# A bidirectional gated recurrence with fusion and a ternary FFN: the recurrent part's fixed slots become a list-scheduled graph of tasks

## Chip, cores and metric

One core of one Trainium2 chip runs the whole kernel in one launch. The metric is device time in microseconds (us), the median of several executions. The engines are named as in the profile: PE (TensorE matmul) and PEld (its weight load), DVE (VectorE), ACT (ScalarE), POOL (GpSimd) and SP (SyncE, which issues most DMAs).

## What is computed

Eight batches of 512 tokens with 512 features, fp32. A four-layer gated recurrence (forward and backward, with the same weights), a fusion of both directions, a residual, then an FFN with ternary weights:

```python
def _mingru(x, Wz, bz, Wh, bh):
    z = jax.nn.sigmoid(jnp.einsum('bsi,hi->bsh', x, Wz) + bz)
    h_tilde = jnp.tanh(jnp.einsum('bsi,hi->bsh', x, Wh) + bh)
    a = jnp.clip(1.0 - z, CLAMP_LO, CLAMP_HI)
    return _linear_scan(a, z * h_tilde)
...
    for i in range(L):
        h_new = _mingru(h, Wz[i], bz[i], Wh[i], bh[i])
        if i > 0:
            h_new = h_new + h
        h = _layernorm(h_new, gamma, beta)
...
h_fwd = _stack(x, ...)
h_bwd = jnp.flip(_stack(jnp.flip(x, axis=1), ...), axis=1)
return jnp.einsum('bsi,hi->bsh', jnp.concatenate([h_fwd, h_bwd], -1), fusion_W) + fusion_b
...
# FFN: absmean(W) is W made ternary (-1, 0, 1) at half the mean of abs(W)
h = jax.nn.gelu(jnp.einsum('btd,hd->bth', x, absmean(W_fc)), approximate=False)
h = layernorm(h, ln_w, ln_b)
return jnp.einsum('bth,dh->btd', h, absmean(W_proj))
...
x = x + recurrent(layernorm(x))
x = x + ffn(layernorm(x))
```

The call passes one weight for `Wz` and `Wh` and for both directions (`ctx_1024`) and one bias (`cond_1024`), so one product serves the sigmoid and the tanh, and layer 0's product serves both directions.

## The kernel before

**Layout.** Within the recurrence a state is held with features on partitions: four tiles of 128 features by 512 tokens. A *gate* is one such output tile: four fp32 matmuls (L487; L535 for layer 0), accumulated in one PSUM bank `u`. From `u`, ACT makes `a` (sigmoid of the negated sum), `t` (tanh) and `z` (sigmoid), L505 to L507; POOL clamps `a` (L511); DVE multiplies `z` by `t` (L514), runs the scan along the tokens (L518) and from layer 1 on adds the old state (L588, L594).

**Layer norm.** It needs rows, so each of four token tiles is turned (four transposes, L316) into a bank `pt`. DVE finds mean and variance (L171, L173), adds epsilon (L177), negates the mean (`nmu`, L182); POOL raises to the power -1/2 (L178); ACT makes `nmr` = -mean times that power (L188) and writes the normalised rows `tok` (L189). When the four are there, four groups of transposes turn them back (L325, bank `pf`) and ACT applies gamma and beta (L331). Of the last layer only the statistics are needed (`rsv`), since the norm is folded into the fusion weights `fw`; of three of its sixteen sequences ACT finds them in two passes (L396, L398). The norm of the input is likewise folded into layer 0: its rows give a scale per token (`rx`, then `scale` by way of `pr`, L385), which DVE multiplies into `u` (L546).

**Fusion.** For a token tile, four matmuls for each direction into `pu` (L622), two evictions by DVE that scale and add to the residual row (L632), and a store to `x1` in DRAM.

**Order.** Batches go in pairs. Within a pair, layers 1 to 3 run over (first batch, forward), (first, backward), (second, forward), (second, backward), four gates each. The fusion tiles of a pair alternate with the layer-0 gates of the next. The order of everything around the gates is written out by hand as *slots*: `slot` (one gate or one fusion tile) issues its matmuls, then what is due of `stages` (factors, clamps, scans, sums) and shares of the queues `turns` and `backs` (transposes and what follows them). How late a step comes is a count of slots. Each engine carries out its own instructions in the order in which they were issued. PSUM's eight banks are divided: four for `u` and `pu`, two for `pt`, two for `pf`.

**Side work.** While the first pair runs, both FFN weights are read in 32 parts, summed in absolute value by ACT (L653), read again, made ternary by DVE (L193, L194) and stored; they come back as `fcq` and `pwq` at the end of the recurrent part. `fold_sums`, `fold_parts`, `fold` and `fold_bias` put gamma, beta and the mean into `fw` and `fb`.

**FFN.** For each batch 16 chunks of 128 hidden features: eight matmuls into `ph` (L910), gelu, square and a split into `ghi` and `glo` (ACT and DVE, L914 to L927), and two chunks later eight matmuls into `po` (L937). The next batch's rows are read, their statistics found (`stats`) in chunks 6 and 7, normalised in 8 and 9 and turned in the last four.

Of the kernel before, what the change touches and what calls it, by code (L numbers as in the profile page):

```python
# [12 lines left out]
ALU = mybir.AluOpType  # L13
# [11 lines left out]
def kernel(  # L25
# [17 lines left out]

# [9 lines left out]
    ZT = 16  # L61
    TOK = 10

    const = ctx.enter_context(tc.tile_pool(name="const", bufs=1))
    small = ctx.enter_context(tc.tile_pool(name="small", bufs=8))
    wpool = ctx.enter_context(tc.tile_pool(name="wts", bufs=1))
    hp = ctx.enter_context(tc.tile_pool(name="h", bufs=6))
    dram = ctx.enter_context(tc.tile_pool(name="x1", bufs=1, space=bass.MemoryType.DRAM))

    tokp = ctx.enter_context(tc.tile_pool(name="tok", bufs=TOK))  # L70
    xsp = ctx.enter_context(tc.tile_pool(name="xs", bufs=12))
    zp = ctx.enter_context(tc.tile_pool(name="z", bufs=ZT))
    ps_f = ctx.enter_context(tc.tile_pool(name="ps_f", bufs=2, space=PSUM))
# [4 lines left out]
    stgp = rec.enter_context(tc.tile_pool(name="stg", bufs=3))  # L78
    qp = rec.enter_context(tc.tile_pool(name="quant", bufs=2))


# [5 lines left out]
    x1 = [[dram.tile([P, H], F32, tag=f"x1_{b}_{t}", name=f"x1_{b}_{t}") for t in range(NT)] for b in range(B)]  # L87


    gw = [wpool.tile([P, NC_, H], F32, tag=f"w{l}", name=f"gw{l}") for l in range(L)]  # L90

    xs = {}

    def load_x(use, b, t):
        xs[use, b, t] = xsp.tile([P, H], F32, tag="xs", name=f"x{use}_{b}_{t}")
        nc.sync.dma_start(out=xs[use, b, t], in_=x[b, ts(t, P), :])

    def load_gw(l):
        nc.sync.dma_start(out=gw[l], in_=gru_wT[l].rearrange("(c p) h -> p c h", p=P))

    xT = {}

    def load_xT(b):
        xT[b] = hp.tile([P, NC_, S], F32, tag="h", name=f"xT_{b}")
        nc.sync.dma_start(out=xT[b], in_=xt[b].rearrange("(c p) s -> p c s", p=P))
# [15 lines left out]
    for i in range(2):  # L121
        plain = tokp.tile([P, H], F32, tag="tok", name=f"plain{i}")[:, 0:P]
        nc.vector.memset(plain, 0.0)
        nc.vector.memset(plain[64 * i : 64 * i + 1, :], 1.0 / H if i else 1.0)
        s = fusp.tile([P, P], F32R, name=f"fpick{i}")
        nc.vector.tensor_copy(s, plain)
        picks.append(s)


    xT[0] = hp.tile([P, NC_, S], F32, tag="h", name="xT_0")  # L130
# [4 lines left out]
    def first_xT(q, c):  # L135
        q.dma_start(out=xT[0][:, c, :], in_=xt[0][ts(c, P), :])

    def first_rows(q, t):
        xs["n", 0, t] = xsp.tile([P, H], F32, tag="xs", name=f"xn_0_{t}")
        q.dma_start(out=xs["n", 0, t], in_=x[0, ts(t, P), :])  # L140
# [10 lines left out]
    for t in range(NT):  # L151
        load_x("n", 1, t)
    load_xT(1)
# [3 lines left out]
    for l in range(1, L):  # L157
        load_gw(l)
# [7 lines left out]
    ngb = const.tile([P, L, NC_], F32, name="ngb")  # L166

    def stats(src, name, rs=None, shift=True):

        st = small.tile([P, 6], F32, tag="st", name=f"st_{name}")  # L170
        nc.vector.bn_stats(st, src)  # L171
        mv = small.tile([P, 2], F32, tag="mv", name=f"mv_{name}")
        nc.vector.bn_aggr(mv, st)  # L173
        if rs is None:
            rs = small.tile([P, 1], F32, tag="rs", name=f"rs_{name}")
        ve = small.tile([P, 1], F32, tag="ve", name=f"ve_{name}")
        nc.vector.tensor_scalar(ve, mv[:, 1:2], LN_EPS, None, ALU.add)  # L177
        nc.gpsimd.tensor_tensor(rs, ve, mhalf, ALU.pow)  # L178
        if not shift:
            return rs, None  # L180
        nmu = small.tile([P, 1], F32, tag="nmu", name=f"nmu_{name}")
        nc.vector.tensor_scalar(nmu, mv[:, 0:1], -1.0, None, ALU.mult)  # L182
        return rs, nmu

    def normalise(dst, src, rs_nmu, name):
        rs, nmu = rs_nmu
        nmr = small.tile([P, 1], F32, tag="nmr", name=f"nmr_{name}")
        nc.scalar.activation(nmr, nmu, AF.Copy, scale=rs)  # L188
        nc.scalar.activation(dst, src, AF.Identity, bias=nmr, scale=rs)  # L189

    def ternary(dst, w, hi_lo):

        nc.vector.tensor_scalar(dst, w, hi_lo[1], None, ALU.is_lt)  # L193
        nc.vector.scalar_tensor_tensor(dst, w, hi_lo[0], dst, ALU.is_gt, ALU.subtract)  # L194

    def fc_part(i):

        return fc_wT[ts(i % NC_, P), ts(i // NC_, 512)]

    def proj_part(i):  # L200
        return proj_wT[ts(i, P), :]

    def load_y(b):

        for t in range(NT):
            xs["y", b, t] = xsp.tile([P, H], F32, tag="xs", name=f"xy_{b}_{t}")
            nc.sync.dma_start(out=xs["y", b, t], in_=x1[b][t])

    ys = {}

    def y_chunk(b, toks, c, px):

# [3 lines left out]
        def split():  # L216
            hi = zp.tile([P, S], F32R, tag="z", name=f"yhi_{b}_{c}")
            lo = zp.tile([P, S], F32R, tag="z", name=f"ylo_{b}_{c}")
            nc.scalar.copy(hi, px)
            nc.vector.tensor_tensor(lo, px, hi.bitcast(F32), ALU.subtract)  # L220
            ys.setdefault(b, []).append((hi, lo))
        return split

    NW = NQ * NC_
    fcq, pwq = [], []
    rows = {}


    with rec:
        gp = rec.enter_context(tc.tile_pool(name="gate", bufs=3))  # L230
        ps_u = rec.enter_context(tc.tile_pool(name="ps_u", bufs=4, space=PSUM))
        ps_t = rec.enter_context(tc.tile_pool(name="ps_t", bufs=2, space=PSUM))


        nc.scalar.activation(warm, warm, AF.Sigmoid)

        now = [0]
        state = {}
        rsv = {}
        turns, backs = [], []  # L240

        held = [0]

        class Tokens(list):


            lag = 1

            def append(self, tile_):
                super().append(tile_)  # L250
                self.at = now[0] + self.lag

        def ready(at):
            if isinstance(at, Tokens):
                return len(at) == NT and at.at <= now[0]
            return at <= now[0] and held[0] < TOK

        def shares(cap):


            last = []
            for q in (turns, backs):
                some = []
                for i in range(max(2, cap)):
                    if not q or not ready(q[0][0]):
                        break
                    at, piece = q[0][:2]
                    late = (at.at if isinstance(at, Tokens) else at) + piece <= now[0]
                    if i >= cap and not late:
                        break  # L270
                    some.append(take(q))
                last = some + last
            return last

        zlive = [0]

        left = {}

        def queue(q, key, at, piece, go):
            left[key] = left.get(key, 0) + 1  # L280
            q.append((at, piece, key, go))

        def take(q):
            _, _, key, go = q.pop(0)
            left[key] -= 1
            return go()

        def need(*keys):

            while any(left.get(k) for k in keys):  # L290
                slot(None, 2)

        def tokens(source, tok, rs, name):

            def go():
                src = source()
                found = stats(src, name, rs, tok is not None)
                if tok is None:
                    return lambda: None
                held[0] += 1  # L300

                def last():
                    tile_ = tokp.tile([P, H], F32, tag="tok", name=f"tok_{name}")
                    normalise(tile_, src, found, name)
                    tok.append(tile_)
                return last
            return go

        def turned(zs, t, name, frees=0):
            def source():  # L310
                if t == NT - 1:
                    zlive[0] -= frees
                spare = name.startswith("00_0") and t > 1
                pt = (ps_f if spare else ps_t).tile([P, H], F32, tag="pf" if spare else "pt", name=f"pt_{name}")
                for c in range(NC_):
                    nc.tensor.transpose(pt[:, ts(c, P)], zs[c][:, ts(t, P)], ident)  # L316
                return pt
            return source

        def back(toks, dst, c, affine, name):  # L320

            def go():
                pf = ps_f.tile([P, S], F32, tag="pf", name=f"pf_{name}")
                for t in range(NT):
                    nc.tensor.transpose(pf[:, ts(t, P)], toks[t][:, ts(c, P)], ident)  # L325
                if c == NC_ - 1:
                    held[0] -= NT
# [524 lines left out]
        load_pw(3)  # L852

# [239 lines left out]
```

## Time and profile before

| | |
|---|---|
| median of three runs | 1712.43 us (1712.39 to 1712.62) |
| the profiled execution: device time | 1712.95 us |
| its span, first to last instruction | 1711.2 us |
| first gate starts | 8.71 us |
| first FFN matmul starts | 1217.46 us |
| busy: DVE / ACT / POOL | 1389.1 / 1089.5 / 377.2 us |
| gates of layers 1 to 3 (L487), busy | 345.5 + 345.5 us |
| fusion matmuls (L622), busy | 115.2 + 115.1 us |

The span is what the trace shows of one execution; the device time has a little around it. A window line gives a stretch's start and end, its length, and for each engine the busy time and the number of instructions (in brackets), then the granted PE clock, the share of the DMA engines and GB/s. A wait line gives the waiting engine, the tile it works on and its line, what released it, and then the sum in us, the number of waits and the longest. In a timeline the two numbers ahead of the engine are start and duration in us; matmuls overlap in the pipeline, so the distance of starts, not the duration, is their pace.

### The profile page before, as it was taken

Reading aid. Unit: us, or ns where it says so; the run is one execution under the profiler, and the core shown is the slowest. Engines: PE = TensorE matmul, PEld = TensorE weight load, DVE = VectorE, ACT = ScalarE, POOL = GpSimd, SP = SyncE. Lnnn points to the kernel's source line nnn. Section 1 sums busy time; section 2 is a strip of 40 time slices with the busy share of each in tenths; the row PEclk is TensorE's granted clock in tenths of the full one; section 3 lists DMA queues with packets and bytes.
Section 4 is the critical chain, followed back from the end, with each engine's and each line's share of the span. In section 5 each row is a group of like instructions: output and inputs, shape, how many; then the busy total and the mean of one; then the engine's idle time right before and its main releaser. Section 6 shows DMA issues by size and latency. Waiting matters only on the chain.

```text
span 1711.2 us, 19776 instructions
## 1 busy us (share of the span) xinstructions
PE 1700.3 (99%) x6440; PEld 1042.6 (61%) x6440; DVE 1389.1 (81%) x2619; ACT 1089.5 (64%) x1918; POOL 377.2 (22%) x558
## 2 busy tenths in 40 slices
PE   9999999999999999999999999999999999999999
PEld 5455554555555455555545555554688888888887
DVE  7988889889887888888788888885568768768877
ACT  5898873468886346888535688862356566666654
POOL 3333333223332222333222222321000000000000
PEclk9999999999999999999999999999999999999999
DMA  7002231150000125000012200102201101100100
GB/s 271 19 25 81 98 93 37 66 193 19 13 1 1 56 68 191 19 13 1 1 56 75 98 28 22 75 1 99 74 1 50 50 1 50 50 21 30 50 19 31
DMA packets 46599, 91.75 MB, mean 54 GB/s; under 512 B 5280, under 2 KB 5536, under 8 KB 45472
## 3 DMA queue, kind: packets, MB, share of 16 engines
q1 hardware_dynamic: 45488, 88.78, 15.1%
q10 hardware_dynamic: 1008, 1.70, 0.3%
q8 instruction: 51, 0.84, 0.2%
q14 instruction: 52, 0.43, 0.1%
HBM read 65.30 MB, written 25.17 MB: 53 GB/s over the span
## 4 chain that ended last, share of the span: by engine, by line
PE 92%; DVE 5%; ACT 2%; POOL 1%; issue 0%; DVEq 0%
PE u L487 33%; PE po L937 14%; PE ph L910 14%; PE pu L622 13%; PE u L535 6%; PE pt L316 6%; PE pf L325 4%; DVE z L518 1%; PE py L214 1%; DVE z L514 1%; DVE st L171 1%; ACT tok L189 1%; DVE z L588 1%; PE pst L948 0%; POOL rs L178 0%
## 5 line engine op out<-in xcount | busy, mean ns | idle before, releaser
L487 PE MATMUL u<-xT,gw 128*128 128x512 f32 x768 | 345.5, 593 | 0.0
L487 PE MATMUL u<-h,gw 128*128 128x512 f32 x768 | 345.5, 592 | 0.0
L518 DVE TENSOR_TENSOR_SCAN z<-a,z 128x512 f32<-128x512 f32 x224 | 277.1, 1237 | 21.8 <-DVE z L514 0.9
L511 POOL TENSOR_SCALAR a<-a 128x512 f32<-128x512 f32 x224 | 150.3, 671 | 559.2 <-ACT a L505 558.3
L487 PEld LDWEIGHTS u<-xT,gw 128*128 128x128 f32 x768 | 138.6, 190 | 138.7 <-issue 137.0
L487 PEld LDWEIGHTS u<-h,gw 128*128 128x128 f32 x768 | 138.6, 190 | 138.2 <-issue 138.2
L505 ACT ACTIVATE a<-u,ngb 128x512 f32<-128x512 f32 x192 | 131.7, 686 | 142.4 <-PE u L487 140.9
L937 PE MATMUL po<-pwq,ghi 128*128 128x512 f32 x512 | 202.8, 396 | 0.0
L171 DVE BATCH_NORM_STATS2 st<-pt 128x6 f32<-128x512 f32 x244 | 169.3, 694 | 39.2 <-PE pt L316 32.5
L937 PE MATMUL po<-pwq,glo 128*128 128x512 f32 x512 | 199.7, 390 | 0.0
L910 PE MATMUL ph<-yhi,fcq 128*128 128x512 f32 x512 | 199.7, 390 | 0.0
L910 PE MATMUL ph<-ylo,fcq 128*128 128x512 f32 x512 | 199.4, 389 | 0.0
L514 DVE TENSOR_TENSOR z<-z,t 128x512 f32<-128x512 f32 x224 | 154.8, 691 | 52.6 <-ACT z L507 52.3
L914 ACT ACTIVATE g<-ph 128x512 f32<-128x512 f32 x128 | 76.4, 597 | 186.6 <-PE ph L910 186.6
L178 POOL TENSOR_TENSOR rs<-ve,mhalf 128x1 f32<-128x1 f32 x192 | 125.5, 654 | 155.1 <-DVE nmu L182 152.7
L189 ACT ACTIVATE tok<-pt,nmr,rs 128x512 f32<-128x512 f32 x192 | 149.4, 778 | 6.4
L925 DVE TENSOR_TENSOR acc<-acc,g 128x512 f32<-128x512 f32 x112 | 77.4, 691 | 85.0 <-ACT g L914 84.1
L507 ACT ACTIVATE z<-u,gb 128x512 f32<-128x512 f32 x192 | 132.4, 690 | 0.0
L506 ACT ACTIVATE t<-u,gb 128x512 f32<-128x512 f32 x192 | 130.8, 681 | 0.0
L316 PEld LDWEIGHTS pt<-ident,z 128*128 128x128 f32 x640 | 78.7, 141 | 77.2 <-issue 48.9
L535 PE MATMUL u<-xT,gw 128*128 128x512 f32 x256 | 114.8, 593 | 0.8 <-DVE gw L767 0.8
L622 PE MATMUL pu<-fw,xT 128*128 128x512 f32 x256 | 115.2, 593 | 0.0
(164 smaller groups left out, 2621.0 us busy)
## 6 DMA issues: line engine op xcount, KB each, us to landing
xf<-in_x_dram SPq DMA_DIRECT2D x32, 256.0 KB, 5.5
x<-xf SPq DMA_DIRECT2D x32, 256.0 KB, 2.0
xy<-x SPq DMA_DIRECT2D x32, 256.0 KB, 4.0
xn<-in_x_dram SPq DMA_DIRECT2D x31, 256.0 KB, 4.5
out_dram<-xy SPq DMA_DIRECT2D x31, 256.0 KB, 2.0
xT<-in_xt_dram SPq DMA_DIRECT2D x7, 1024.0 KB, 7.7
fca<-in_fc_wT_dram SPq DMA_DIRECT2D x16, 256.0 KB, 2.9
pwa<-in_proj_wT_dram SPq DMA_DIRECT2D x16, 256.0 KB, 2.6
```

The source lines that it names most:

```text
L171: nc.vector.bn_stats(st, src)
L189: nc.scalar.activation(dst, src, AF.Identity, bias=nmr, scale=rs)
L316: nc.tensor.transpose(pt[:, ts(c, P)], zs[c][:, ts(t, P)], ident)
L487: nc.tensor.matmul(u, lhsT=gw[l][:, c, ts(o, P)], rhs=h[:, c, :], start=(c == 0), stop=(c == NC_ - 1),)
L507: nc.scalar.activation(z, u, AF.Sigmoid, bias=gb[:, l, o : o + 1])
L511: engine.tensor_scalar(a, a, CLAMP_HI, CLAMP_LO, ALU.min, ALU.max)
L514: nc.vector.tensor_tensor(z, z, t, ALU.mult)
L518: nc.vector.tensor_tensor_scan(dst[:, d], a[:, d], z[:, d], 0.0, ALU.mult, ALU.add)
L535: nc.tensor.matmul(u, lhsT=gw[0][:, c, ts(o, P)], rhs=xT[b][:, c, :], start=(c == 0), stop=(c == NC_ - 1),)
L622: nc.tensor.matmul(pu, lhsT=hs[d][:, c, ts(t, P)], rhs=fw[:, d * NC_ + c, :], start=(c == 0), stop=(c == NC_ - 1),)
L910: nc.tensor.matmul(ph, lhsT=w, rhs=ys[b][c][i], start=(c == 0 and i == 0), stop=(c == NC_ - 1 and i == 1),)
L937: nc.tensor.matmul(po[b][t], lhsT=part[:, ts(t, P)], rhs=pwq[k // NP_][:, k % NP_, :], start=(k == 0 and i == 0), stop=(k == NF - 1 and i ...
```

## The change

The hand-written slots are gone. Every step of the recurrent part is made as a `Task` with an engine, the time for which it occupies it (`occ`), the time until its result is there (`lat`), a due time, the tasks it depends on and the buffers it uses. Then `schedule` walks through an estimated time and issues, again and again, the task that can start earliest on any engine, and of those of one engine that can start then, the one with the earliest due time. Buffers are named slots that are claimed when a task is placed: 16 `z`, 10 `tok`, 12 `xs`, 6 `h`, 3 `a`, 2 `t` and so on as before, but the eight PSUM banks are one kind, `ps`. The nominal times `nom` follow the old order of gates and fusion tiles.

```diff
+    class Task:
+        def __init__(self, eng, occ, lat, due, go, deps=(), bufs=(), early=1e9):
+            self.eng, self.occ, self.lat, self.due, self.go = eng, occ, lat, due, go
+            self.rel = max(0.0, due - early)
...
+        def enter(task):
+            r = task.rel
+            for d, off in task.deps:
+                r = max(r, d.start + (d.lat + (0.04 if d.eng == task.eng else 0.09) if off is None else off))
+            task.ready = r
+            cands[task.eng].append(task)
...
+                    r = room(task)
+                    if r is None:
+                        continue
+                    st = max(clock[e], task.ready, r)
+                    some.append((st, task.due, task))
+                    low = st if low is None else min(low, st)
...
+                best = min((s for s in some if s[0] <= low + 0.01), key=lambda s: s[1])
...
+            task.start = st
+            clock[task.eng] = st + task.occ
...
+            task.go()
```

A gate is four PE tasks (`matmuls`), one ACT task for the three factors, one POOL and two or three DVE tasks; a group of four transposes is one PE task:

```diff
+                last = Task("PE", 0.86, 1.08, due + 0.86 * c, go, [*deps(c), last and (last, 0.86)], [u, *bufs])
...
+            act = Task("ACT", 1.74, 1.84, due + 3.6, go, deps, [*bufs, a, t, z])
+            cl = Task("POOL", 0.64, 0.66, due + 3.6, lambda: nc.gpsimd.tensor_scalar(a.tile, a.tile, CLAMP_HI, CLAMP_LO, ALU.min, ALU.max), [(act, 0.75)], [a])
+            pr = Task("DVE", 0.62, 0.70, due + 5.5, lambda: nc.vector.tensor_tensor(z.tile, z.tile, t.tile, ALU.mult), [act], [z, t])
...
+            return pt, Task("PE", 0.44, 0.66, due, go, deps, [pt, *zs])
...
+                due = min(end + 4.3 + 4.3 * t, nxt - 16.0 + 2.0 * t)
+                pt, tr = turned(zs, t, name, due, ends)
+                st = stat("VVVV"[t], lambda pt=pt: pt.tile, pt, m, t, due + 1.0, [tr], [pt])
+                pw = pows(m, due + 1.5, [st], t)
+                sh = Task("DVE", 0.07, 0.13, due + 2.0, lambda t=t: shifted(m.tile, t), [pw], [m])
...
+                due = min(end + 21.5 + 4.3 * c, nxt - 5.0 + 0.86 * c)
...
+        pieces(60.0, 170.0, 900.0)
...
+        schedule(dict(PE=8.7, ACT=11.9, DVE=12.5, POOL=13.7, SP=26.0))
```

What else differs:

- The statistics of one norm lie in one small tile. `nmu` (DVE) and `nmr` (ACT) are replaced by `shifted`, one DVE instruction after POOL's power, in the recurrent part and in the FFN (`stats`, `normalise`):

```diff
-        nmr = small.tile([P, 1], F32, tag="nmr", name=f"nmr_{name}")
-        nc.scalar.activation(nmr, nmu, AF.Copy, scale=rs)
-        nc.scalar.activation(dst, src, AF.Identity, bias=nmr, scale=rs)
+        nc.gpsimd.tensor_tensor(m[:, 9:10], m[:, 8:9], mhalf, ALU.pow)
+        nc.vector.scalar_tensor_tensor(m[:, 10:11], m[:, 0:1], -1.0, m[:, 9:10], ALU.mult, ALU.mult)
+        nc.scalar.activation(dst, src, AF.Identity, bias=m[:, 10:11], scale=m[:, 9:10])
```

- Last norms: DVE finds all statistics (`"VVVV"`). Input rows of batches 1 to 7: two tiles by DVE, two by ACT (`"VVAA"`), and one power for the four tiles. A statistic by ACT has one instruction more (the variance).
- Before the first gate's result is scaled, the statistics of batch 0 are all issued ahead of the four powers, and gamma and beta are copied into `both`.
- DMAs are tasks on SP with due times; row loads may be issued up to 30 us before they are due, and the weights of the FFN when their slots come free.
- A second form of the norm that goes by way of DRAM (`rows_norm`) is in the code, but `by_rows` returns False.
- After the recurrent part `ps_f` is a new pool of two banks, and the FFN's `z`, `tok` and `xs` tiles go round the slots in a ring.

## Prediction

> **What bounds the kernel now.** I read the page first, then busy time by stretches, the timeline of one layer, and what TensorE (PE) waited for.
>
> The page: sums and granted clock.
>
> ```profile
> span 1711.2 us, 19776 instructions
> ...
> PE 1700.3 (99%) x6440; PEld 1042.6 (61%) x6440; DVE 1389.1 (81%) x2619; ACT 1089.5 (64%) x1918; POOL 377.2 (22%) x558
> ...
> PEclk9999999999999999999999999999999999999999
> ```
>
> PE is busy 99% at full clock. But its ends are modelled, so I count the matmuls. The timeline of a layer gives their pace:
>
> ```profile
> 500.71 3.60 PE L487 MATMUL u<-xT,gw 128*128 128x512 f32 x8
> 504.14 0.60 PE L316 MATMUL pt<-ident,z 128*128 128x128 f32 x4
> 504.58 0.60 PE L325 MATMUL pf<-ident,tok 128*128 128x128 f32 x4
> 505.02 3.60 PE L487 MATMUL u<-xT,gw 128*128 128x512 f32 x8
> ```
>
> The first column is the start. A gate (four fp32 matmuls, two records each) takes 504.14 - 500.71 = 3.43 us, four transposes 0.44. The page and its longer list give, for the recurrent part, 768+768+256+256+256+16 records of 128x512, so 290 fours, and 1024+768+32+16 transposes, so 460 fours; the few others sum to 2.5. That is 290 x 3.43 + 460 x 0.44 + 2.5 = 994.7 + 202.4 + 2.5 = 1199.6 us. The first gate starts at 8.71 and the first FFN matmul at 1217.46: 1208.8 us. So PE loses only about 9.2 us in the part that changes, and nothing in the change can win more. Where do they lie?
>
> ```profile
> core 0: us, PE busy (x) PEld busy (x) DVE busy (x) ACT busy (x) POOL busy (x), PEclk, DMA share, GB/s
> 8.70:100.00 91.30, 88.97 (x316) 46.74 (x317) 81.79 (x162) 72.69 (x138) 32.97 (x46) 1.00 0.32 111
> 100.00:262.00 162.00, 160.62 (x585) 86.64 (x584) 140.64 (x275) 134.96 (x257) 58.91 (x80) 1.00 0.24 78
> ...
> 662.00:860.00 198.00, 197.61 (x720) 106.28 (x719) 170.66 (x331) 150.25 (x257) 63.44 (x98) 1.00 0.09 31
> ```
>
> Visible idle of PE: 91.30 - 88.97 = 2.33 us up to 100, 1.38 up to 262, 0.39 in the layers of each of the two middle pairs, 0.82 in those of the last: 5.3 in all. The other 3.9 hide behind modelled ends. Spread in proportion, the first 100 us hold 2.33 x 9.2/5.3 = 4.0. The steady part is nearly perfect. What PE waits for there:
>
> ```profile
> engine line waited for: us in total, times, longest us
> PE pt L316 <- ACT tok L189: 2.6, 6, 0.9
> PE pf L325 <- ACT tok L189: 1.0, 3, 0.4
> ```
>
> In all 3.6 of the 5.3. The first row is transposes that want a `pt` bank, of which there are two, each held until ACT has normalised from it. ACT and DVE are full in that stretch:
>
> ```profile
> 45.00:60.00 15.00, 14.47 (x56) 7.63 (x55) 12.93 (x20) 14.84 (x25) 4.37 (x7) 1.00 0.00 0
> 60.00:75.00 15.00, 15.00 (x44) 6.95 (x42) 14.21 (x22) 9.28 (x19) 4.62 (x5) 1.00 0.11 36
> 75.00:90.00 15.00, 13.61 (x59) 7.84 (x58) 13.99 (x34) 13.94 (x27) 6.46 (x9) 1.00 0.06 17
> ```
>
> **A rule against this reading.** The Trainium skill (Perfetto Trace Analysis, Identifying the Most-Contended Engine) says that matmul busy time is a bad measure of headroom and weight-load time a better one. By that, with PEld at 61%, 39% of the span, 667 us, would be the ceiling on a gain; by the pace above it is 9.2. The pace is this case's own, and I go by it.
>
> **The change, part by part** (against the profiled execution: span 1711.2, its device time 1712.95, so 1.75 around it; it stands 0.5 above the median 1712.43, and I subtract from the median).
>
> *PE work.* The same gates, transposes, fold matmuls and preamble up to 8.71: 0.
>
> *The eight banks become one pool*, taken oldest first, so a transpose no longer waits for one of two `pt` banks. *The normalising step* loses its ACT instruction `nmr` (192 x 0.30 = 57.8 us by its row; four in each layer of some 17 us, 7% of ACT) to a DVE instruction that replaces `nmu` (0.14) one for one. *The absolute sums*, 32 ACT passes of 0.63, get due times from 60 to 170 us and stop competing with the first layers. All this attacks the 9.2.
>
> *The start.* What may remain there lies between 0 and 4.0, plus up to 0.7: one added ACT step in each of two statistics (0.20 each) and all four variances put ahead of the powers delay the first scale row; POOL's four powers at 0.55 began at 11.5 and PE waited 0.2 for them at 13.7, now they begin near 12.2. DVE is 90% busy from 30 to 105, so not all can be had; ACT's relief says not none. I take 2.0.
>
> *Tight picks.* The old order put transposes a fixed number of slots after their data; the list scheduler takes them at the first decision of PE after its estimate says ready. A decision falls every 0.86 us (one matmul), so the cover is even between 0 and 0.86. Each of 48 layer norms has two such picks (first turn, first turn back) and each of 16 last norms one: 112. What can be late are POOL's steps:
>
> ```profile
> L178 POOL TENSOR_TENSOR rs<-ve,mhalf x192: 550/551/1457, 33.1 to 1118.3; 128x1 f32<-128x1 f32 x192
> ...
> L178 POOL TENSOR_TENSOR rx<-ve_x,mhalf x28: 550/928/930, 11.5 to 804.8; 128x1 f32<-128x1 f32 x28
> ```
>
> (min/median/max ns.) The scheduler counts 0.62 to 0.66. A slowed one takes some 0.93, 0.38 longer; the page's mean of 654 puts their share at (654 - 550)/378 = 28%. Lateness 0.38 against an even cover costs 0.38 x 0.38/(2 x 0.86) = 0.084; x 28% x 48 turns back = 1.1, and with a restart of 0.06 for five of them 1.4 us. The first turns hang on the clamp (POOL, 0.61, mean 0.67, longest 1.59), which runs beside ACT's two other factors and the product: it ends at 0.76 + 0.61 = 1.37 after the first factor's start; the third factor starts at 1.16, the product 0.72 later, the scan 0.78 after that, at 2.66 (distances in the timeline). Cover 1.3, so 0. If queueing ate that cover, 0.98 of lateness costs 0.56, x 64 x 9% (the share that its mean gives) = 3.2. So 0 to 4.6, I take 1.4.
>
> The Trainium skill (SBUF — State Buffer, Who interferes with whom) makes this worse than even odds: VectorE and GpSimd share a port pair under an exclusive lock and the loser fully blocks. The trace has both sides (0.55 and 0.98 for the same power). By the rule every power or clamp that meets a two-input DVE instruction would wait; at 100% in place of 28% the turns back cost 4, not 1.1.
>
> *DVE now waits for POOL* inside its own queue (the shift comes after the power: 0.08 + 0.55 + 0.03 of idle). Behind it stand products, scans and sums of other gates. DVE has 198.0 - 170.7 = 27 us of idle per pair's layers, for 32 such waits of at most 0.66 - 0.07: 19 us if the scheduler filled none. Hidden; if not, it is the slower rival below.
>
> *FFN.* The same shift costs VectorE some 0.8 us more per row tile, four tiles per batch at chunks 6 and 7, ahead of the next `glo`: 3.3 us. In the trace `glo` of chunk 8 of batch 1 ends at 1313.7 and PE wants it at 1317.6: cover 3.9, 0.6 left, so 0; without cover, 7 batches x 0.4 = 2.8.
>
> *Into the FFN.* The first `ph` bank is now one that a fusion tile may just have used: 0 to 1.6 (two evictions of 0.75), two chances in eight: 0.4. SP's loads of rows, xT and weights keep their number; they are sent up to 30 us ahead and land in 4 to 8, 1 MB weights in 16: 0.
>
> *Moved statistics*: 12 tiles of last norms from ACT (1.6 each) to DVE (0.73 + 0.22), 12 of x from DVE to ACT: cancel.
>
> **Sum**: 1712.4 - 9.2 + 2.0 + 1.4 + 0.4 = 1707.0.
>
> **Rivals.** (1) *Slower: the tight picks miss.* VectorE's queue is in order and 86% full; a late power at its head passes the delay to every later product, so lateness isn't 28% of 48 but general. It decides from a mean stall of (9.2 - 2.0 - 0.4)/112 = 0.06 us per pick; at 0.13, a third of one slowed power, 14.6 us go: 1712.4 - 9.2 + 2.0 + 14.6 + 0.4 = 1720.2. For it: the old steady part loses 0.4 per 200 us and can only get worse; POOL's 1.59. Against: rows as given, the estimates lie within some 0.05 us. Chance 0.29.
> (2) *No change: the start is bound by VectorE*, 4.0 + 0.7 remain, and the turns cost 3.2 more than nothing: 1712.4 - 9.2 + 4.7 + 3.2 + 0.4 = 1711.5. For it: DVE 14.21 of 15 us at 60 to 75. Chance 0.26.
> (3) *The schedule isn't what it says*: a room rule (16 `z`, six `h`) blocks a gate of 3.43 once in each pair: +13.7, 1720.7; counted in (1).
>
> **Chances and range.** About 0.2% (3.4 us) is what a measurement can tell. Forecast (faster) 0.45, same 0.26, slower 0.29. Its own range is 1704 to 1709. The range reaches from 1704 (1712.4 - 9.2 and rounding) to 1721, which leaves out under 0.2: larger stalls.
>
> **What would show it.** Right: PE's visible idle between 8.7 and 100 under 1.2 us, no wait of a `pt` transpose on ACT's `tok` there, ACT under 14.5 of 15 us from 45 to 60; the first FFN matmul near 1212. Wrong: many transposes with 0.1 to 0.5 us of idle behind ACT or DVE in 364 to 1159, POOL's powers with a median over 0.8, idle on PE at `po` of chunks 7 to 9. Gates that stand in the old order with the old stalls would show that nothing moved.

## The result, and the profile after

| | median of the runs, us | range | profiled execution: device time, span |
|---|---|---|---|
| before | 1712.54 (8 runs) | 1712.39 to 1713.09 | 1712.95, 1711.2 |
| after | 1717.03 (8 runs) | 1716.19 to 1719.52 | 1717.4, 1715.6 |

After to before is 1.0027, 95% interval 1.0016 to 1.0038: slower by 0.27%, 4.5 us. The forecast was 1707.0, faster.

The page after: span, then busy time of each engine with its share and number of instructions.

```profile
span 1715.6 us, 19179 instructions
...
PE 1703.3 (99%) x6440; PEld 1043.6 (61%) x6440; DVE 1345.4 (78%) x2598; ACT 1028.8 (60%) x1710; POOL 393.3 (23%) x537
```

TensorE has as many matmuls as before (6440). DVE has 44 us less to do than before, ACT 61 us less. Nothing of that reached the time. As in the prediction, the page's PE share hides what matters, so the loss is taken from starts: the distance from each TensorE instruction's start to the next, less its pace (0.429 us for an fp32 record of 512 columns, 0.109 for a transpose, 0.23 and 0.26 for the twelve others). The work from the first gate to the first FFN matmul is 1198.81 us by that count in both kernels. (In the timeline of before the first FFN matmul starts at 1216.90; the 1217.46 of the table further up is where the critical chain's first piece of the FFN begins.)

| us | before | after |
|---|---|---|
| first gate starts | 8.71 | 9.02 |
| lost up to 110 us | 4.63 | 10.02 |
| lost from 110 us to the first FFN matmul | 4.75 | 3.76 |
| first FFN matmul starts | 1216.90 | 1221.61 |
| from there to the end | 494.27 | 494.01 |

So 5.4 us are lost at the start, 1.0 is won in the steady part, 0.3 in the FFN, and 0.3 goes on a first gate that started later. The stretches of after say the same (us of the stretch, then busy us of PE, PEld, DVE, ACT and POOL, each with its number of instructions, the granted clock, DMA share, GB/s):

```profile
core 0: us, PE busy (x) PEld busy (x) DVE busy (x) ACT busy (x) POOL busy (x), PEclk, DMA share, GB/s
30.00:45.00 15.00, 11.34 (x39) 7.58 (x38) 9.48 (x23) 5.95 (x10) 3.37 (x6) 0.77 0.69 243
45.00:60.00 15.00, 14.55 (x52) 7.55 (x51) 14.45 (x32) 14.46 (x26) 5.48 (x8) 1.00 0.00 1
60.00:75.00 15.00, 13.89 (x67) 8.20 (x66) 14.81 (x32) 14.81 (x32) 5.26 (x8) 1.00 0.11 36
364.00:562.00 198.00, 198.00 (x716) 106.01 (x715) 166.77 (x323) 139.35 (x222) 70.56 (x91) 1.00 0.13 43
```

Before, the same stretch from 30 to 45:

```profile
30.00:45.00 15.00, 15.00 (x62) 8.49 (x61) 13.44 (x32) 9.54 (x18) 4.79 (x7) 1.00 0.35 129
```

From 30 to 45 us every engine does less than before: PE has 39 instructions where it had 62, DVE 9.48 us of work where it had 13.44, and the granted clock is 0.77. In a steady layer (364 to 562) PE has no visible idle at all. What PE waits for from 110 us to the FFN, before (first fence) and after (second), confirms the steady part: the waits of transposes on ACT's `tok`, for a bank, are gone.

```profile
PE pt L316 <- ACT tok L189: 1.2, 3, 0.4
PE pth_fc L664 <- DVE tot_fc L658: 0.7, 1, 0.7
PE pf L325 <- ACT tok L189: 0.7, 2, 0.4
PE py L214 <- DVE ylo L220: 0.4, 1, 0.4
```

```profile
PE pt L517 <- DVE z L610: 0.9, 2, 0.5
PE pf L543 <- ACT tok L534: 0.4, 1, 0.4
```

The standstill itself, in VectorE's timeline of after (start, duration, engine, line, operation; in brackets the idle before it and what ended it):

```profile
30.01 0.66 DVE L492 TENSOR_TENSOR z<-u,scale 128x512 f32<-128x512 f32 x1
36.01 0.69 DVE L306 BATCH_NORM_STATS2 mx<-xn 128x6 f32<-128x512 f32 x1 [5.35 <-DMA xn<-in_x_dram]
36.74 0.18 DVE L307 BATCH_NORM_AGGREGATE mx<-mx 128x2 f32<-128x6 f32 x1
36.84 0.66 DVE L471 TENSOR_TENSOR z<-z,t 128x512 f32<-128x512 f32 x1
```

At the head of VectorE's queue stands the statistic of an input row of batch 2, and the row has not landed. It is not urgent: the scale that comes of it is written at 128 us and first used at 281, some 245 us later. But the change gives this statistic a due time of 36.2 us, the nominal start of layer 1 of the first pair. Behind it stand the product, the scan and all else of the layer that runs. TensorE follows:

```profile
35.13 0.49 PE L517 MATMUL pt<-ident,z 128*128 128x128 f32 x3
39.28 4.74 PE L517 MATMUL pt<-ident,z 128*128 128x128 f32 x21 [3.66 <-DVE z L476]
```

It stands for 3.66 us, and then takes 4.74 us for 21 transposes that need 2.3 at the pace. Why the row is late is in the DMA view from 24 to 37 us: the queue's packets, MB and share of the 16 engines, and, for SP's row loads, number, KB each and median time from issue to landing.

```profile
q1 hardware_dynamic: 2744, 4.76, 101.5%
...
xn<-in_x_dram SPq DMA_DIRECT2D x7, 256.0 KB, 9.4
```

The queue is full of the fusion and gate weights (2 MB and three of 1 MB, issued from 13 to 22 us; the last of them lands at 35.2). The row was issued at 25.74 and landed at 35.99. The scheduler takes SP as free at 26.0 and counts 3.93 us for 256 KB, so it had the row there at 29.9, and it put the statistic where VectorE, by its estimate, had nothing better: at 30.

### The profile page after: what moved, and what is told of

Read it like the earlier page. It is cut to its first block, busy times and chain, and to the rows that moved or that the text cites. A ratio compares the mean times of both kernels' runs of the same rounds, so it can differ in the third digit from the quotient of the medians.

```text
span 1715.6 us, 19179 instructions
## 1 busy us (share of the span) xinstructions
PE 1703.3 (99%) x6440; PEld 1043.6 (61%) x6440; DVE 1345.4 (78%) x2598; ACT 1028.8 (60%) x1710; POOL 393.3 (23%) x537
## 4 chain that ended last, share of the span: by engine, by line
PE 83%; DVE 7%; ACT 5%; DMA 2%; POOL 1%; issue 1%; SPq 1%; ACTq 0%; DVEq 0%; POOLq 0%
PE u L458 33%; PE po L965 14%; PE ph L938 14%; PE pu L458 13%; PE pf L543 4%; PE pt L517 4%; DVE z L476 2%; PE pt L635 2%; DVE z L471 1%; POOL m L329 1%; DVE m L306 1%; ACT tok L534 1%; ACT a L466 1%; DVE z L610 1%; ACT z L468 1%
## 5 line engine op out<-in xcount | busy, mean ns | idle before, releaser
L476 DVE TENSOR_TENSOR_SCAN z<-a,z 128x512 f32<-128x512 f32 x256 | 313.1, 1224 | 7.2
L458 PEld LDWEIGHTS u<-xT,gw 128*128 128x128 f32 x1024 | 185.9, 191 | 192.7 <-issue 184.3
L470 POOL TENSOR_SCALAR a<-a 128x512 f32<-128x512 f32 x224 | 162.6, 726 | 494.7 <-ACT a L466 492.0
L329 POOL TENSOR_TENSOR m<-m,mhalf 128x1 f32<-128x1 f32 x256 | 192.5, 755 | 284.9 <-DVE m L321 262.3
L534 ACT ACTIVATE tok<-pt,m 128x512 f32<-128x512 f32 x192 | 147.0, 787 | 141.5 <-DVE m L332 123.8
L306 DVE BATCH_NORM_STATS2 m<-pt 128x6 f32<-128x512 f32 x256 | 175.0, 684 | 15.8 <-PE pt L517 14.4
L543 PEld LDWEIGHTS pf<-ident,tok 128*128 128x128 f32 x768 | 92.6, 141 | 68.0 <-issue 57.9
L517 PEld LDWEIGHTS pt<-ident,z 128*128 128x128 f32 x768 | 93.3, 143 | 45.2 <-issue 29.1
L517 PE MATMUL pt<-ident,z 128*128 128x128 f32 x768 | 113.6, 277 | 4.7 <-DVE z L476 3.7
```

The source lines that it names most:

```text
L306: nc.vector.bn_stats(own(m, t, 0, 6), src)
L329: nc.gpsimd.tensor_tensor(one(m, t, Col.RS), one(m, t, Col.VE), mhalf, ALU.pow)
L458: nc.tensor.matmul(u.tile, lhsT=lhs(c), rhs=rhs(c), start=(c == 0), stop=(c == NC_ - 1))
L470: cl = Task("POOL", 0.64, 0.66, due + 3.6, lambda: nc.gpsimd.tensor_scalar(a.tile, a.tile, CLAMP_HI, CLAMP_LO, ALU.min, ALU.max), [(act, 0 ...
L476: nc.vector.tensor_tensor_scan(dst[:, d], a[:, d], z[:, d], 0.0, ALU.mult, ALU.add)
L517: nc.tensor.transpose(pt.tile[:, ts(c, P)], zs[c].tile[:, ts(t, P)], ident)
```

## The experiments

Each is compared with before, measured beside it at 1712.51 to 1712.64. Diffs are against after. Losses are those of the one profiled execution, by the count above.

### Is it the late row?

**e1_estimate** moves one start value of the estimate, so that rows are expected 6 us later:

```diff
-        schedule(dict(PE=8.7, ACT=11.9, DVE=12.5, POOL=13.7, SP=26.0))
+        schedule(dict(PE=8.7, ACT=11.9, DVE=12.5, POOL=13.7, SP=32.0))
```

> The scheduler's SyncE starts at 32 in place of 26, so that its estimate of the first prefetched row of batch 2 (30 us) moves to where that row landed (36.0). Theory A (VectorE stood 5.3 us at the head of its queue for a row that came late, PE lost 3.8 us behind it and then ran at half clock for 5.9 us, some 2.8 us more): both go, 1717.0 - 6.6 = 1710.4, between 1709 and 1712; no wait of VectorE on that row. Theory B (the start is bound by VectorE's work, the late row only shows where): the loss comes back elsewhere before 110 us and the time stays over 1715.

Measured: 1712.57, ratio 1.0 (0.9991 to 1.0009), 4.5 us less than after. The wait on the row falls from 5.3 to 0.3. But the estimate changes the whole order, and of the 4.5, 1.8 came beyond 110 us. So a second experiment leaves the order of PE, DVE, ACT and POOL as it is.

**e3_row_early** only loads that one row sooner: its DMA goes ahead of the fusion weights, and its place in the schedule issues nothing.

```diff
+    nc.sync.dma_start(out=xrow["n", 2, 0].claim(), in_=x[2, ts(0, P), :])
...
+            if (use, b, t) == ("n", 2, 0):
+                return dma(due, 256, lambda: None, (), [buf], 30.0)
```

> Every engine's order as in the changed kernel; only the first row tile of batch 2 is loaded ahead of the fusion and gate weights, so it lands near 21 us in place of 36. Theory A: VectorE no longer waits at 30.7, PE doesn't stall at 35.2, clock stays full: 1717.0 - 6.6 = 1710.4 (1709 to 1712). Theory B: over 1715.

Measured: 1712.87, ratio 1.0001 (0.9992 to 1.001). VectorE's timeline of it, the same four instructions:

```profile
30.90 0.66 DVE L495 TENSOR_TENSOR z<-u,scale 128x512 f32<-128x512 f32 x1
31.48 0.68 DVE L307 BATCH_NORM_STATS2 mx<-xn 128x6 f32<-128x512 f32 x1
32.20 0.18 DVE L308 BATCH_NORM_AGGREGATE mx<-mx 128x2 f32<-128x6 f32 x1
32.30 0.66 DVE L474 TENSOR_TENSOR z<-z,t 128x512 f32<-128x512 f32 x1
```

The order is the same and the 5.35 are gone. The loss up to 110 us falls from 10.02 to 6.08, the loss beyond it stays (3.73 for 3.76). The four engines run the same instructions in the same order as in after. The earlier load even makes the rows of batch 1 land later, and the first factor start at 18.70 in place of 17.81. The gain is not the clock's alone: at a granted clock of 0.999 e3 takes 1713.35 to 1714.26 (five executions), after 1716.19 to 1716.81 (four). This shows the cause of 4 us: one row, behind the weights. Both runs exclude theory B and end a little above the range of theory A, 1709 to 1712. Of the standstill and the half clock behind it (below) only 4 us come back, because TensorE now waits elsewhere:

```profile
41.26 0.66 PE L520 MATMUL pt<-ident,z 128*128 128x128 f32 x4 [0.29 <-ACT tok L537]
43.85 1.13 PE L461 MATMUL pfold<-fw,both 128*128 128x512 f32 x2 [1.94 <-ACT tok L537]
```

**e2_clock_kept** asks whether it was the standstill or the clock after it. It leaves the late row and lets TensorE run 17 matmuls that nobody reads in the gap:

```diff
+                    if name == "00_0_0" and c == NC_ - 1:
+                        for _ in range(17):
+                            nc.tensor.matmul(pt.tile[:, ts(c, P)], lhsT=ones, rhs=ones, start=True, stop=True)
```

> The order of the changed kernel, with 17 idle matmuls (0.21 us each) put between the third and the fourth transpose of the first turn, where PE stood still. VectorE waits as before. Theory A with the clock as a cost of its own: no stretch at half clock near 38 us, 1717.0 - 2.8 = 1714.2. If the lower clock costs nothing because PE catches up: 1717.

Measured: 1718.05, ratio 1.0031 (1.0019 to 1.0042): nothing gained. TensorE's timeline:

```profile
35.35 3.96 PE L519 MATMUL pt<-ones 128*128 128x128 f32 x34
39.15 2.46 PE L520 MATMUL pt<-ident,z 128*128 128x128 f32 x21
...
47.44 1.12 PE L458 MATMUL pfold<-fw,both 128*128 128x512 f32 x2 [1.93 <-ACT tok L537]
```

The 21 transposes now take 2.46 us in place of 4.74, and the granted clock is 1.00 from 30 to 45. By 44.67 us of after e2 is 2.80 us ahead. Then the time saved goes into a wait of 1.93 for ACT's `tok`, where after waited 0.4: at that `pfold` e2 is 0.91 ahead, and 0.91 is what its row happened to land earlier (VectorE and ACT run 0.91 ahead all the way from 36 to 57 us). So nothing is left of the clock that was kept; it was cover for VectorE and ACT.

The total says less, because e2 did not keep its clock to the end: after the wait of 1.93 the granted clock is 0.50 from 48.8 to 52.3 us. The same two `pfold` records there, in e2 and in after:

```profile
48.84 1.90 PE L458 MATMUL pfold<-fw,both 128*128 128x512 f32 x2
49.75 1.02 PE L458 MATMUL pfold<-fw,both 128*128 128x512 f32 x2
```

By 52.24 us e2 is 0.75 behind after: this second stretch at half clock, which nothing covers, costs some 1.6 us.

### What else is lost at the start?

In after ScalarE's scale copy, which the first gate's products need, starts at 15.40, and the first factor at 17.81. Before, they started at 14.20 and 15.54. In between ScalarE works on statistics of batch 1, of some 1.9 us each. ScalarE's timeline of after, shortened to one statistic and its two neighbours:

```profile
15.40 0.57 ACT L449 COPY scale<-pr 128x512 f32<-128x512 f32 x1
15.86 0.63 ACT L312 ACTIVATE xn<-xn 128x512 f32<-128x512 f32 x1
...
17.81 0.71 ACT L466 ACTIVATE a<-z,ngb 128x512 f32<-128x512 f32 x1
```

Not all of it is theirs: in e5 below, without them, the scale copy still starts at 15.02. A task that may be early is taken whenever it can start first, and nothing takes the engine from it when the urgent one comes. **e5_act_held** is e1 with those statistics held until they are due, **e7_held_alone** the same on after:

```diff
-                st.append(stat("VVAA"[t], lambda row=row: row.tile, row, m, t, dues[t], [done["xn", b, t]], [row], 30.0))
+                st.append(stat("VVAA"[t], lambda row=row: row.tile, row, m, t, dues[t], [done["xn", b, t]], [row], 0.0 if b == 1 else 30.0))
...
-        norm_x(1, [13.0, 14.0, 18.0, 22.0], nom["l0", 1, 0] - 3.0)
+        norm_x(1, [13.0, 14.0, 20.0, 24.0], nom["l0", 1, 0] - 3.0)
```

> The run with the corrected estimate (1712.6), and the two statistics of batch 1 that ScalarE makes are held back to 20 and 24 us, behind the first two gates' factors. Theory C (what is left of the loss at the start comes from these statistics, which the scheduler put ahead of the first factors because ScalarE was free: first factor at 18.7 in place of 15.5 us, 3.1 us passed on down VectorE's chain): first factor near 15.6, 2 to 3 us less, 1709.5 to 1710.6. Theory B (the start is bound by VectorE's work): no change, 1712.6.

> The changed kernel with the statistics of batch 1 held back alone, the estimate of the late row left as it was (26). VectorE's order still has that row early, so it waits until it lands (near 36). Theory A and C together: the row hides the gain, 1716 to 1717.5. If the statistics alone were the cause: 1713.

Measured: e5 1711.86, ratio 0.9999 (0.9991 to 1.0008); e7 1716.65, ratio 1.0022 (1.0013 to 1.0031). In e5 the first factor starts at 16.36:

```profile
15.02 0.59 ACT L449 COPY scale<-pr 128x512 f32<-128x512 f32 x1 [2.65 <-PE pr L447]
16.36 0.72 ACT L466 ACTIVATE a<-z,ngb 128x512 f32<-128x512 f32 x1 [0.76 <-DVE z L492]
```

That is 1.6 us earlier than in e1 (17.99), and by the medians it is worth 0.7 (e5 against e1) and 0.4 (e7 against after), where theory C wanted 2 to 3. Both lie inside the intervals, so that it helps is not shown by the times. In e7 a row still holds VectorE for 3.7 us.

**e8_calibrated** is e5 with the other start values of the estimate set by the traces of the changed kernel's runs (arrivals of xT, weights and rows, the first scale, and the clocks `PE=8.7, ACT=12.4, DVE=13.0, POOL=14.6, SP=32.0`).

> The run with the statistics held back (1711.9), and the scheduler's starting values are those that the traces of the changed kernel show: engines free at 12.4 (ACT), 13.0 (DVE) and 14.6 us (POOL), the first scale's powers at 14.5, the transposed input at 10.0 and 11.7, gate weights at 28.6 to 35.3, fusion weights at 26.0. The arithmetic and the parts are the same. If the loss at the start is a matter of wrong estimates: PE's loss from the first gate to 110 us falls from 6.3 to 3 or 4, 1709. If it is VectorE's and ScalarE's work: over 5.5 and 1711.5 to 1712.5.

Measured: 1710.87, ratio 0.999 (0.9981 to 0.9999), between what the two explanations wanted. The loss up to 110 us is 4.51, that of before (4.63), for 6.31 in e5; beyond it the loss is 3.32 for 2.50.

### Are the shared banks worth anything?

**e4_banks_split** is e1 with the eight PSUM banks divided as before: four for gates and fusion, two for `pt`, two for `pf`.

```diff
+    banks = {"ps": (4, 5, 6, 7), "pt": (0, 1), "pf": (2, 3)}
+    free.update({k: [(0.0, f"ps{i}") for i in n] for k, n in banks.items()})
...
+            if kind == "ps" and name[:2] in ("pt", "pf", "pr", "py") and not name.startswith(("pth", "pfold")):
+                kind = "pt" if name[:2] == "pt" else "pf"
```

> As the run with the corrected estimate, but the eight PSUM banks are divided as before the change: four for gates and fusion, two for turns, two for turns back. If the common pool is what removed the old waits of turns on ScalarE's rows (3.6 us visible), this is 2 to 4 us slower than that run; if the due times and the lighter ScalarE did it, within 1 us.

Measured: 1717.91, ratio 1.0033 (1.0022 to 1.0045), 5.3 us above e1. What PE waits for in e4:

```profile
PE pt L521 <- ACT tok L538: 5.4, 4, 3.2
PE pt L521 <- DVE z L614: 1.3, 4, 0.6
```

The wait for a `pt` bank that the prediction named is back, all of it before 110 us, and larger than before (2.6). That is what the prediction said the one pool takes away. The size is not the banks' alone: the schedule made with divided banks has another order too.

### Is ScalarE's work in the first 100 us movable?

**e6_act_relief** is e5 with the absolute sums due later, `pieces(110.0, 200.0, 900.0)` for `pieces(60.0, 170.0, 900.0)`, and the statistics of batches 2 and 3 due one layer later.

> As the run with the statistics held back, and the absolute sums of the FFN weights start at 110 in place of 60 us and the rows of batches 2 and 3 go through their statistics one layer later, so that ScalarE (14.5 to 14.9 of 15 us busy from 45 to 105) is relieved. Theory D (from 45 to 105 the start is bound by ScalarE): another 1 to 2 us less, near 1708.5. If VectorE binds it: no change.

Measured: 1720.55, ratio 1.0048 (1.0035 to 1.006), 8.7 slower than e5, which neither explanation had. The loss up to 110 us does fall, from 6.31 to 4.75, but beyond it the loss rises from 2.50 to 11.93. The largest waits that are new:

```profile
PE u L458 <- ACT tok L534: 2.5, 1, 2.5
PE pth_fc L682 <- DVE tots_fc L680: 2.2, 1, 2.2
```

They lie at 331 and 295 us, in the fusion stage of the first pair, where the postponed work now ends. **e9_sums_later** is e8 with the sums moved by 25 us only, `pieces(85.0, 170.0, 900.0)`; **e12_rows_later** is e11 (below) with the rows of batches 2 and 3 one layer later.

> As the calibrated run, and the absolute sums start at 85 in place of 60 us, but end by 170 as before. If ScalarE is what is short from 45 to 105: 1 to 2 us less than the calibrated run, with PE's loss up to 110 under 3. If not, the same within 0.7.

> As the run with the fold later, and the statistics of the rows of batches 2 and 3 are due one layer later as well. If work of VectorE and ScalarE binds the stretch: up to 1 us less again, 1707.5 to 1708.5; else no change.

Measured: e9 1712.63, ratio 0.9997 (0.9989 to 1.0006), 1.8 above e8; e12 1709.9, ratio 0.9984 (0.9975 to 0.9993), 1.5 above e11. Neither helps. In e9 more is lost up to 110 us (6.12 against 4.51) though ScalarE has less to do there (85.8 us against 89.6). The order changes as a whole, a wait of the fold's mean on ScalarE grows from 1.7 to 2.4, and behind it the profiled execution of e9 has 3.4 us at a granted clock of 0.50 that e8's has not.

### Do the picks come too tight, and what else fills the first 90 us?

**e10_later_picks** is e8 with a margin on what TensorE waits for from other engines:

```diff
-                r = max(r, d.start + (d.lat + (0.04 if d.eng == task.eng else 0.09) if off is None else off))
+                r = max(r, d.start + (d.lat + (0.04 if d.eng == task.eng else 0.40 if task.eng == "PE" else 0.09) if off is None else off))
```

**e11_fold_later** adds to it that the second half of the fold (copy, remainder, mean, bias) is due 80 us later. One line of six that change alike:

```diff
-                hc = Task("ACT", 0.60, 0.70, dues[d] + 8.0, lambda whole=whole, hi=hi: nc.scalar.copy(hi.tile, whole.tile), [cp], [whole, hi])
+                hc = Task("ACT", 0.60, 0.70, dues[d] + 88.0, lambda whole=whole, hi=hi: nc.scalar.copy(hi.tile, whole.tile), [cp], [whole, hi])
```

> As the calibrated run, but the scheduler counts 0.40 in place of 0.09 us from another engine's result to PE, so that PE picks a group of transposes later. If tight picks cost something in the steady part, PE's loss from 110 us to the FFN falls from 2 or 2.5 to under 1.2 and the time by about 1 us; if they cost nothing, no change.

> As the run with later picks (1710.1), and what follows the two fold sums (their split, the means, the eight changes of the fusion weights and the bias) is due 80 us later, out of the stretch from 45 to 105 us in which VectorE and ScalarE are 95 to 99% busy. If that stretch is bound by these two engines' work: PE's loss up to 110 falls from 5.1 to 3 or 3.5 and the time to 1708.5. If the loss there is a matter of order alone: no change.

Measured: e10 1710.05, ratio 0.9982 (0.9973 to 0.9991), 0.8 below e8; e11 **1708.45**, ratio 0.9975 (0.9966 to 0.9985), faster than both kernels: 4.2 us below before, 8.6 below after. With the margin the loss beyond 110 us falls from 3.32 to 2.01, and up to 110 it rises from 4.51 to 5.07. With the fold moved, the wait of its mean goes: it was 1.7 us, PE's longest in e10.

```profile
PE pm L726 <- ACT z L468: 1.7, 1, 1.7
```

In e11 3.12 are lost up to 110 and 2.21 beyond, 5.3 where before lost 9.4. The intervals of the two single steps overlap, but the granted clock of the single executions tells them apart. Behind the wait of 1.7 the profiled execution of e10 has 3.4 us at a clock of 0.50; e11's, with a wait of 1.1, has none (PEclk is the third number from the end; e10, then e11):

```profile
60.00:75.00 15.00, 13.27 (x51) 7.55 (x50) 14.79 (x36) 14.34 (x31) 5.95 (x8) 0.89 0.27 88
60.00:75.00 15.00, 13.90 (x59) 7.81 (x58) 14.63 (x39) 14.97 (x31) 6.89 (x10) 1.00 0.12 36
```

| granted clock over the execution | e8 | e10 | e11 |
|---|---|---|---|
| 1.000 | 1710.18 to 1711.24 (7) | 1708.79 to 1708.95 (5) | 1708.31 to 1708.98 (8) |
| 0.999 | 1711.73 to 1712.03 (4) | 1710.05 to 1710.73 (6) | 1708.39 (1) |

At full clock the margin (e8 to e10) is worth 1.4 us by the medians, with no overlap, and the later fold 0.3. (In e11's profiled execution, the one at 0.999, the clock falls only in the last 2 us.) So, as far as these readings tell, most of e11's 1.6 against e10 is the clock that it does not lose behind that wait. (One execution of each kernel is traced; that the others at 0.999 lost it in the same place is inferred.) That VectorE and ScalarE were relieved is not the reason shown: from 8.7 to 110 us ScalarE is busy 91.2 us in e11 and 89.5 in e10, VectorE 89.9 and 93.5. The time and the loss came as expected; the explanation that they were expected from did not show.

## Why the prediction was right or wrong

**The steps that failed: SP's loads, put at 0, and the start, put at 2.0.** The loads first: "SP's loads of rows, xT and weights keep their number; they are sent up to 30 us ahead and land in 4 to 8, 1 MB weights in 16: 0." The number was right, and the DMAs had been counted, but the 4 to 8 were the landing time of rows elsewhere in the trace. At 25.7 us the queue holds megabytes of weights: 9.4 us was the median for the seven row loads there, 10.25 for the first. The trace of before had this figure, for three loads of the same size in the same stretch (24 to 37 us):

```profile
fca<-in_fc_wT_dram SPq DMA_DIRECT2D x3, 256.0 KB, 9.2
```

And the price is not the lateness of a row that is used 245 us later. It is what stands behind the row's statistic in VectorE's in-order queue: 5.35 us of wait, 4 us of time (e3). The prediction asked who waits behind POOL's powers in that queue, and did not ask it of a DMA. It also left unchecked the `SP=26.0` in the change's last line and the landing time that the schedule counts for a row, 3.93 us.

**The sum.** Of the 10.0 us between 1707.0 and 1717.0, 8.0 lie in the term for the start (10.0 lost for 2.0), 2.0 beyond 110 us (3.76 for 1.8), 0.3 in a first gate that came later, and -0.3 in the FFN.

**The start: 2.0 (0 to 4.0 + 0.7) measured 10.0.** Without the late row 6.1 remain (e3), still above the range. Statistics by ScalarE put ahead of the first factors may be a part of it: the prediction gave 0.7 for the first scale row as an upper bound, and the first factor came 2.27 us later than before (17.81 against 15.54). The prediction had counted the instructions added to each statistic, and not that whole statistics of the next batch would be put ahead. What that costs in time no run shows. The end of its range was also the old loss, on the ground that less ScalarE work can only help; a new order can lose more than the old.

**Rival 2's mechanism, a start bound by VectorE, is open for what is left.** The windows of after show DVE and ACT at 14.81 of 15 us from 60 to 75. Postponed work lowered the loss up to 110 us in e6, from 6.31 to 4.75, and raised it in e9 and e12 (to 6.12 from 4.51, to 3.88 from 3.12). Better start values alone (e8) brought it from 6.31 to 4.51, and most of e11's gain seems to be the clock. How much of e11's remaining 3.1 us is too much work and how much is order is not shown. Rival 3, a gate blocked once in each pair, did not come: in the layers of the later pairs TensorE shows no idle time from 364 to 562, 0.09 us from 662 to 860 and 1.24 from 960 to 1159.

**The banks: right.** The waits of `pt` on ACT's `tok` are gone, and come back with split banks: 5.4 us of wait, and a time 5.3 us longer (e4), where 2 to 4 were expected.

**Tight picks and the way into the FFN, 1.4 and 0.4: right in kind, too small.** 3.76 us are lost beyond 110 us where 1.8 were predicted. Of these 2.4 stand ahead of first turns, for which the prediction took 0, and 1.2 ahead of turns back, for which it took 1.4. Against e8 the margin of e10 takes 1.3 away. That this was tightness is not shown: e1, without a margin, loses 1.96 there, so another order does as much. Rival 1, which wanted 0.06 us and more at each of 112 picks, 6.7 us in all, did not come: the new kernel was slower by another mechanism, one that no rival named. The median power by POOL stayed at 0.55:

```profile
L329 POOL TENSOR_TENSOR m<-m,mhalf x256: 543/551/1524, 43.0 to 1186.5; 128x1 f32<-128x1 f32 x128
```

but the mean is 0.755, so by the prediction's own sum (755 - 551)/378 = 54% were slowed and not 28%. Counted in the trace, 115 of the 256 took 0.59 us or more, 45%, and 18 of them some 1.52; before it was 45 of 192, 23%. The rule on the port pair that the prediction weighed, by which all that meet would be blocked, is not borne out as a count of all, but the share did rise. One sum of the prediction is off here: for the clamps, (671 - 614)/980 gives 6% and not 9%, so 2.1 us in place of 3.2, and 1710.4 for rival 2.

**DVE's waits for POOL: right, hidden.**

```profile
DVE m L332 <- POOL m L329: 23.8, 53, 1.5
```

19 us for each pair's layers had been given for it if nothing was filled; 23.8 came in the whole kernel, in 53 waits behind 192 powers, and TensorE shows no idle time in the steady layers (364 to 562).

**FFN: right.** 494.01 us from its first matmul to the end, before 494.27. Of the cover of 3.9 at chunk 8, 0.6 was to be left; in five of the batches 0.56 or 0.57 is left and in one 0.26, and TensorE waits for no `glo`.

**The ceiling: right.** 9.2 was to be had at most; the best kernel here has 4.2 of it. Two small errors cancel in the 9.2: 0.44 for four transposes is 0.436, and the 1217.46 is 1216.90. By the starts it is 9.4. That the weight-load share would leave 667 us, as the rule weighed in the prediction has it, found no support: no run came below 1708.31.

**The signs to look for.** Visible idle from the first gate to 100 us was to be under 1.2 and is 90.98 - 85.75 = 5.23; the first FFN matmul was to come at 1212 and came at 1221.6 (in e11 1212.55). These two were wrong and told it at once. No wait of `pt` on `tok`, ACT at 14.46 of 15 from 45 to 60, POOL's median, no idle at `po`: all as forecast, and none of them sees the standstill.

## What to carry to other kernels

When an order is made from estimates, look first at the estimates of what comes from outside, the DMAs, in the stretch where the queue is fullest, and ask for each early load what stands behind its first reader on an in-order engine: a row needed 245 us later cost 4 us. Look for a landing time in the same stretch and not for a median of the whole trace. A task that can wait needs a due time that says so: here the row's statistic was due at 36 us. To test such a cause, change the arrival and leave the order (e3): a changed estimate changes everything. When single executions differ in their granted clock, compare those that agree in it.

## What was not expected of the hardware

- **A standstill of TensorE can halve its clock; whether that costs time depends on what covers it.** After 2.3 us of the standstill of 3.66 us the granted clock went to 0.50, and stayed there until 44.8 us:

```profile
37.00:38.00 1.00, 0.00 (x0) 0.00 (x0) 1.00 (x2) 0.00 (x0) 0.00 (x0) 0.97 0.99 354
38.00:39.00 1.00, 0.00 (x0) 0.00 (x0) 1.00 (x2) 0.81 (x2) 0.01 (x1) 0.50 0.86 260
...
44.00:45.00 1.00, 1.00 (x3) 0.40 (x2) 0.97 (x4) 0.83 (x2) 0.97 (x2) 0.62 0.00 0
```

  That is 5.5 us of work at half clock from 39.28 on, 2.7 us by the pace; in e2, which has full clock there, nothing of it was left at 47.44, since TensorE waited as long for ACT. The Trainium skill (TensorE: Matmul & The Clock Gate, HAM oscillation — how this bites in real kernels) reckons the penalty as the throttled time by one minus the clock's ratio. For the 6.8 us from 37.9 to 44.8 that would be an estimate of 3.4, for a stretch of 3.4 us 1.7. Where nothing covers the stretch the runs come near it: 1.6 in e2 (48.8 to 52.3 us), and 1.5 between the medians of e10's executions with 0.999 and with 1.000. In the first stretch of after the sum is an upper bound, because other engines were late as well.
- **Which wait is followed by half clock is not plain from its length.** A wait of 1.93 us was in e2, one of 1.94 in e3 was not; 1.7 was in the profiled execution of e10 and not in that of e8; e10 has executions at both readings of the clock. Each of these stretches near the start lasted 3.4 us, in after 6.8.
- **A row of 256 KB takes 10.25 us behind the rest of 5 MB of weights in one queue,** and SP's row loads a median of 3.7 in the first 24 us of the same execution.
- **The first gate starts between 8.40 and 9.06 us** in the profiled executions of kernels whose code up to there is nearly the same. In after and e1, where it is the same, the four `pm` matmuls ahead of it take 2.75 and 2.38 us. Some 0.4 us of a difference between two profiles is of this kind.
